# An output projection of 20 products of 171 columns in place of seven of 256, with new TensorE lists

## The chip, the cores and the metric

The kernel runs on one core of a Trainium2 chip. The metric is the time of one execution on the device in microseconds; the time of a kernel is the median of several runs. The core has a matrix engine (TensorE, PE in the profile; its weight loads have a row of their own, PEld), three engines for everything else (VectorE, DVE; ScalarE, ACT; GpSimd, POOL) and a queue that issues transfers (SyncE, SP). Each works through its own list of instructions in order and waits for the others by semaphores. [...]

## The reference, cut to what matters

The input x is 128 batches of 128 rows (tokens) and 512 columns, adj is 128 x 128. Layer 0 is a residual step and a norm. Layer 1 is masked attention with eight heads, an output projection and two norms. The change concerns `o @ w_proj + b_proj`:

```python
# layer 0 (W1 = W2 = adj): only the row maximum of A = adj @ x is needed beside x
pre = A[:, :, None, :] + (C - A)[:, :, :, None];  out = max(relu(pre), axis=-1)
x = layernorm(x + out)
# layer 1
qkv = (x @ w_qkv);  attn = softmax(mask(q k^T * scale));  o = attn @ v
o = o @ w_proj + b_proj                   # w_proj: 512 x 512
ln = (o - mean) * rsqrt(var + 1e-5) * gamma + beta
x = layernorm(x + o + ln)
```

All is float32.

## The kernel before

The 128 batches are worked off in 32 groups of four. A loop over p (from line 1482) walks through the groups in a software pipeline: step p does the scores S0 to S3 and the values product V of group p, the attention product A0 to A3 and the output projection O of group p - 1, the query and key product Q of group p + 1, and layer 0's product L of group p + 2. Tokens stand in columns, so a group's projection multiplies a 512 x 512 block (two halves of 256 tokens, four blocks of 128 rows) by a 512 x 512 weight.

Large products are not done plainly. Q and V use tables (`QK` and `VV`) of bilinear schemes: some sums of the left side are made by POOL (`token_sums`, tiles `hl`), the right side is replaced once by combined weights (`weight_forms`, line 776), and the class `Bilinear` (line 893) then runs "nodes". A node multiplies one or two sums by weight forms into a bank, adds earlier snapshots to it (DVE), seeds other banks with a copy of it (ACT, `k<-k`), keeps a snapshot in SBUF (`u<-k`), or writes a block of the result (DVE, the rest by POOL). The values product V takes 20 products of 171 columns, the projection O takes Strassen's seven products of 256 columns (`class Strassen`, `unit_sums`, `o_unit`, tiles `so` for the sums, `wp` for the weights). In O, ACT first copies the bias row into two banks, ACT keeps three snapshots, and DVE writes four result blocks `o`. A product of 171 columns has two matrix multiplications, one of Strassen's has four; in the trace each float32 multiplication is two instructions.

After O, `tails` does both norms of a group: DVE statistics, POOL roots and wide sums, ACT scalings, with the rows `xr` loaded back from memory.

Attention itself uses part of the array: in `scores` an operand has 64 rows (`k<-qk`, 64*128), in `attend` an output has 64 rows (`k<-s,v`, 128*64). All others use the full 128*128.

What sets the order: the lists `FIRST`, `STEP` and `LAST` fix TensorE's order in the first, middle and last step, token by token (`A2` is the attention of batch 2, `V5` node 5 of V, and so on). In `LAST`, B and R are attention and plain projection of the last group and T is the end of the group before it. All other engines' instructions, and SP's transfers, are ordered by a planner (class `Plan`), which has a cost for each operation, gives it a due time from TensorE's ideal times and picks the next one by due time. Buffers have fixed slots; a buffer waits for the readers of the one before it in its slot. `take` hands out the eight banks.

```python
STEP = """
A0 A1 A2 A3 S0 S1 S2 S3 V0 V1 V2 V3 V4 V5 V6 V7 V8 V9 V11 V10 V12 V13 V14 V15 L1 V16 V17 L0 O1 O2 O6
O5 O7 O4 Q0 L3 L2 O3 Q2 Q3 Q1 Q4 Q5 Q6 Q7 Q8 Q9 Q14 Q10 Q11 Q12 Q15 Q13 Q17 Q19 Q20 Q18 Q21 Q23 Q22
Q24 Q16 Q25
""".split()
```

Many helpers record instructions under one line: line 466 is every matrix multiplication, 460 every two-operand sum (DVE or POOL), 463 every scalar-tensor-tensor on DVE. Tile names then tell them apart.

Of the kernel before, what the change touches and what calls it, by code (L numbers as in the profile page):

```python
# [14 lines left out]
AX = mybir.AxisListType  # L15

# [189 lines left out]
)  # L206


STEP = """
A0 A1 A2 A3 S0 S1 S2 S3 V0 V1 V2 V3 V4 V5 V6 V7 V8 V9 V11 V10 V12 V13 V14 V15 L1 V16 V17 L0 O1 O2 O6  # L210
O5 O7 O4 Q0 L3 L2 O3 Q2 Q3 Q1 Q4 Q5 Q6 Q7 Q8 Q9 Q14 Q10 Q11 Q12 Q15 Q13 Q17 Q19 Q20 Q18 Q21 Q23 Q22
Q24 Q16 Q25
# [7 lines left out]

LAST = """
A2 V0 A0 A1 V2 V3 S0 V5 V1 A3 V6 S1 V4 S2 V7 V8 V10 V9 V11 V14 V13 O1 V12 O2 V16 O6 S3 O5 O7 V17 V15
O4 O3 B0 B1 T3 R0 B2 T1 R2 T0 B3 R1 T2 R3
# [12 lines left out]
class Buf:  # L236


    def __init__(self, plan, slot, make):
        self.slot, self.make, self.tile, self.log = slot, make, None, []  # L240
        self.before = plan.slots.get(slot)
        plan.slots[slot] = self
# [143 lines left out]
def kernel(  # L386
# [47 lines left out]
    def take(cols=512, add=False):  # L434


        if cols == 512:
            i = next(i for i in free if not add or i not in partial)
            partial.discard(i)
        else:  # L440
            i = next((i for i in list(free)[:-1] if i in partial), free[0])
            if not add:
                partial.add(i)
        free.remove(i)
        return bank(i)
# [9 lines left out]
    def small(kind, cols, bufs=8):  # L455
        i = small_n[kind] = small_n.get(kind, -1) + 1
        return buf(f"{kind}{i % bufs}", [P, cols])
# [318 lines left out]
    def weight_forms(table, dst, width, block, slots, cost, pool=False):  # L776
        made = {}
        per = 2 * D // width
        rooms = [buf(s, [P, per, width]) for s in slots]

        def operand(i):
            if i < table.blocks:
                return block(i)
            r, c = divmod(i - table.blocks, per)
            return rooms[r], c, lambda: rooms[r].t[:, c]

        def add(dst, dst_at, a, b, sa, sb_):
            (ba, ka, pa), (bb, kb, pb) = a, b
# [19 lines left out]
        def temp(i):  # L808
            if i < table.blocks or i in made:
                return  # L810
            made[i] = True
            a, b, s = table.temps[i - table.blocks]
            temp(a)
            temp(b)
            bt, c, ap = operand(i)
            add(ap, (bt, c), operand(a), operand(b), 1, s)

        for w, terms in enumerate(table.forms):
# [3 lines left out]
            if len(terms) == 1:  # L822
                ((i, s),) = terms
                b, k, ap = operand(i)
# [3 lines left out]
                    lambda ap=ap, form=form, s=s: pin(A.mul(form(), ap(), float(s))),  # L828
# [7 lines left out]
            for i, s in terms[2:]:  # L836
                add(form, at, (dst, w, form), operand(i), 1, s)
# [55 lines left out]
    class Bilinear:  # L893


        def __init__(self, table, left, form, width, rooms, costs, out, on_vector=False):
            self.table, self.left, self.form, self.width = table, left, form, width
            self.on_vector = on_vector
# [3 lines left out]
        def product(self, b, tok, w, start):  # L902
            bt, key, ap = self.left[tok]
# [10 lines left out]
            plan.add("PE", self.costs[0], emit, [(form, w), (bt, key)], [b])  # L914

        def node(self, n):
# [19 lines left out]
            if block is None:  # L936
# [3 lines left out]
                for m in seeds:  # L940
                    nb = self.banks[m] = take(2 * width, True)
                    plan.add("ACT", act, lambda nb=nb: pin(A.copy(cols(nb), cols(b))), [b], [nb])  # L942
# [75 lines left out]

    def weight_load(w, src, col):
        rows = src.rearrange("(d c p) e -> d p c e", d=2, p=P)  # L1020
        for i, d, c in ((0, 0, 0), (3, 0, HE), (1, 1, 0), (2, 1, HE)):
            dma(
                lambda i=i: w.t[:, i],
                lambda d=d, c=c: rows[d, :, :, ds(col + c, HE)],
                [],
                [(w, i)],
                256,
            )

    def weight_sums(w):  # L1030
        for i, a, b in ((4, 3, 0), (6, 2, 3), (5, 2, 4), (3, 1, 5)):
            plan.add(
                "POOL",
                1.3,
                lambda i=i, a=a, b=b: tt(GP, w.t[:, i], w.t[:, a], w.t[:, b], ALU.subtract),
                [(w, a), (w, b)],
                [(w, i)],
            )

    class Strassen:  # L1040


        def __init__(self, w, left, outs, us, bias=None):
            self.w, self.left, self.outs, self.us, self.bias = w, left, outs, us, bias
            self.banks, self.snaps = {}, {}

        def add(self, i, k):
            fresh = False
            if k not in self.banks:
                fresh = self.bias is None or k not in self.bias  # L1050
                b = self.banks[k] = take(add=not fresh)
                if not fresh:
                    src, row = self.bias[k]
                    plan.add("ACT", 0.5, lambda: pin(A.copy(halves(b), row())), [src], [b])
            b = self.banks[k]
            lb, key, ap = self.left[i]
            w = self.w

            def emit():
                left = ap()  # L1060
                for s in range(2):
                    for c in range(2):
                        mm(
                            halves(b)[:, s],
                            left[:, c, ts(s, P)],
                            w.t[:, i - 1, c],
                            fresh and s == 0 and c == 0,
                        )

            plan.add("PE", 1.725, emit, [(w, i - 1), (lb, key)], [b])  # L1070

        def snap(self, k):
            b = self.banks[0]
            u = self.snaps[k] = buf(self.us[k - 1], [P, 512])
            plan.add("ACT", 0.5, lambda: pin(A.copy(u.t, b.t)), [b], [u])

        def result(self, half, col, k, s):
            b, u = self.banks[k], self.snaps[s]
            dst, key, ap = self.outs[half, col]
            plan.add(  # L1080
                "DVE",
                0.61,
                lambda: tt(V, ap(), halves(b), u.t.rearrange("p (k n) -> p k n", k=2), ALU.add),
                [b, u],
                [(dst, key)],
            )

        def product(self, i):
            banks = self.banks
            self.add(i, (None, 0, 1, 2, 3, 2, 0, 0)[i])  # L1090
            if i in (1, 6, 7):
                self.snap((1, 6, 7).index(i) + 1)
            if i == 2:
                self.result(0, 0, 1, 1)
                give(banks[1])
            elif i == 7:
                give(banks[0])
                self.result(1, 1, 2, 3)
            elif i == 3:
                self.result(0, 1, 2, 2)  # L1100
                give(banks[2])
            if i in (4, 7) and 3 in banks and 3 in self.snaps:
                self.result(1, 0, 3, 3)
                give(banks[3])

    def unit_sums(a, s):
        for dst, p, q_, op in (
            (s[0], a[1][0], a[1][1], ALU.add),
            (s[1], s[0], a[0][0], ALU.subtract),
            (s[2], a[0][0], a[1][0], ALU.subtract),  # L1110
            (s[3], a[0][1], s[1], ALU.subtract),
        ):
            plan.add(
                "POOL",
                1.25,
                lambda dst=dst, p=p, q_=q_, op=op: tt(GP, dst[2](), p[2](), q_[2](), op),
                [p[:2], q_[:2]],
                [dst[:2]],
            )
        return {1: a[0][0], 2: a[0][1], 3: s[3], 4: a[1][1], 5: s[0], 6: s[1], 7: s[2]}  # L1120

    def o_unit(g, wp):
        a = [
            [(oT[g, h], None, lambda h=h, d=d: oT[g, h].t[:, ds(2 * d, 2)]) for d in range(2)]
            for h in range(2)
        ]
        rooms = [buf(f"so{i}", [P, 2, 2, HT]) for i in range(2)]
        s = [(rooms[i // 2], i % 2, lambda i=i: rooms[i // 2].t[:, i % 2]) for i in range(4)]
        left = unit_sums(a, s)
        for h in range(2):  # L1130
            os_[g, h] = buf(f"o{h}", [P, 2, D])
        outs = {
            (h, c): (os_[g, h], c, lambda h=h, c=c: os_[g, h].t[:, :, ds(c * HE, HE)])
            for h in range(2)
            for c in range(2)
        }
        bias = {
            0: (bp_bc, lambda: bp_bc.t[:, :HE].unsqueeze(1).to_broadcast([P, 2, HE])),
            2: (bd, lambda: bd.t.unsqueeze(1).to_broadcast([P, 2, HE])),
        }  # L1140
        return Strassen(wp, left, outs, ("u3", "u4", "u5"), bias)
# [177 lines left out]
    def tails(g):  # L1319
        mv = buf(f"mvo{g % 2}", [P, G, 2])  # L1320
        mz = buf(f"mvz{g % 2}", [P, G, 2])
        for j in range(G):
            o = os_[g, j // 2]
            bn(lambda o=o, j=j: o.t[:, j % 2], [o], mv, j)
        stat = finish(mv, range(G))
        rows = []
        for h in range(2):
# [5 lines left out]
            for j in range(2):  # L1333
                norm(
                    lambda z=z, j=j: z.t[:, j],
                    lambda o=o, j=j: o.t[:, j],
# [11 lines left out]
            plan.add("POOL", 2.34, lambda z=z, o=o: tt(GP, z.t, z.t, o.t, ALU.add), [z, o], [z])  # L1348
# [56 lines left out]
    def tail_before(b):  # L1405

        j = b % 2
# [196 lines left out]
```

## Time and profile before

| what | us |
| --- | --- |
| median of 3 runs | 1871.42 (1869.94 to 1871.91) |
| the profiled execution | 1872.38 |
| its span, first to last instruction | 1870.5 |
| PE busy, instructions | 1853.4 (99%), 12013 |
| DVE busy | 1357.2 (73%) |
| ACT busy | 1585.2 (85%) |
| POOL busy | 1440.9 (77%) |
| transfers, mean rate | 183 GB/s |

All times of the trace are counted from the span's start. A line of the timeline gives start, duration, engine, line of the code, operation, output and inputs by tile name, shapes and a count of like instructions that follow each other; a bracket at its end gives idle time ahead of it and what ended that. Matmuls overlap, so the duration of one is longer than the distance to the next. A line of the groups gives busy time and the mean of one.

### The profile page before, as it was taken

The page shows a single profiled execution, that of the slowest core. Times are in us where ns is not written, and L with a number is a line of the kernel's source. Part 1 is how long each engine was busy: PE and PEld are TensorE (multiplying, and loading weights), DVE is VectorE, ACT ScalarE, POOL GpSimd, SP SyncE. Part 2 cuts the span into 40 slices and gives each one's busy share as a digit, 9 for nine tenths or more (in the row PEclk, how much of TensorE's full clock was granted, in tenths as well). Part 3 has the DMA queues.
Part 4 walks back from the last instruction along what each step waited for, and adds up shares of the span by engine and source line. Part 5 has one row for each costly group of instructions (what it writes and reads, how often), then busy time and mean ns, then how long its engine had stood idle before and what let it go on. Part 6 is the DMA issues. An engine that isn't in the chain of part 4 may idle for free.

```text
span 1870.5 us, 37547 instructions
## 1 busy us (share of the span) xinstructions
PE 1853.4 (99%) x12013; PEld 1618.2 (87%) x12013; DVE 1357.2 (73%) x2524; ACT 1585.2 (85%) x4681; POOL 1440.9 (77%) x1546
## 2 busy tenths in 40 slices
PE   9999999999999999999999999999999999999997
PEld 7788988888988889888889888898888888888985
DVE  7677676777776777767777667777677776777668
ACT  4787888988889888889888898888898888988885
POOL 4658877788777788777887777977778877788774
PEclk9999999999999999999999999999999999999999
DMA  7654676557675566765576655667656676557564
GB/s 218 191 161 125 194 212 183 158 168 209 187 209 159 166 189 192 215 172 164 172 204 191 195 160 172 195 186 208 170 165 186 197 198 195 159 168 202 161 223 136
DMA packets 444388, 342.03 MB, mean 183 GB/s; under 512 B 276768, under 2 KB 377248, under 8 KB 444192
## 3 DMA queue, kind: packets, MB, share of 16 engines
q1 hardware_dynamic: 443904, 339.11, 63.2%
q8 instruction: 97, 1.59, 0.4%
q14 instruction: 99, 0.81, 0.1%
q10 hardware_dynamic: 288, 0.52, 0.1%
HBM read 172.82 MB, written 166.72 MB: 182 GB/s over the span
## 4 chain that ended last, share of the span: by engine, by line
PE 95%; ACT 1%; DVE 1%; DMA 1%; POOL 1%; issue 0%; SPq 0%; POOLq 0%; ACTq 0%
PE k L466 95%; DMA xr<-spill 1%; ACT s L1205 0%; ACT s L1234 0%; DVE st L583 0%; POOL xr L460 0%; POOL wqk L460 0%; ACT u L948 0%; ACT k L942 0%; POOL rs L460 0%; ACT xr L654 0%; ACT z L654 0%; DVE k L463 0%; DVE x L460 0%; PE k L728 0%
## 5 line engine op out<-in xcount | busy, mean ns | idle before, releaser
L466 PE MATMUL k<-hl,wqk 128*128 128x256 f32 x2232 | 517.9, 379 | 2.3 <-POOL hl L460 1.3
L466 PEld LDWEIGHTS k<-hl,wqk 128*128 128x128 f32 x2232 | 423.8, 190 | 62.2 <-POOL hl L460 2.4
L1205 ACT ACTIVATE s<-s,nm 128x128 f32<-128x128 f32 x1024 | 400.3, 397 | 2.3 <-DVE nm L1196 2.3
L1234 ACT ACTIVATE s<-s,rec 128x128 f32<-128x128 f32 x1008 | 323.1, 395 | 0.0
L948 ACT COPY u<-k 128x512 f32<-128x512 f32 x551 | 284.1, 529 | 32.3 <-PE k L466 23.3
L942 ACT COPY k<-k 128x512 f32<-128x512 f32 x372 | 192.0, 516 | 137.5 <-PE k L466 129.6
L466 PE MATMUL k<-wv,hl 128*128 128x171 f32 x1736 | 277.4, 310 | 1.1 <-ACT u L948 1.1
L466 PEld LDWEIGHTS k<-wv,hl 128*128 128x128 f32 x1736 | 258.2, 189 | 20.2 <-issue 14.3
L1246 DVE STREAM_TRANSPOSE pu<-s 128x1024 f32<-128x1024 f32 x128 | 159.3, 1245 | 131.9 <-ACT s L1234 131.8
L466 PE MATMUL k<-x1T,wqk 128*128 128x256 f32 x992 | 244.3, 379 | 0.0
L463 DVE SCALAR_TENSOR_TENSOR qk<-k,u 128x512 f32<-128x512 f32 x248 | 169.6, 687 | 101.9 <-PE k L466 48.2
L460 POOL TENSOR_TENSOR x<-x,be_bc 128x1024 f32<-128x1024 f32 x62 | 146.8, 2368 | 108.9 <-DVE xt L689 107.5
L466 PE MATMUL k<-wp,so 128*128 128x256 f32 x992 | 224.6, 379 | 0.0
L466 PEld LDWEIGHTS k<-wp,so 128*128 128x128 f32 x992 | 188.3, 190 | 38.2 <-issue 13.4
L463 DVE SCALAR_TENSOR_TENSOR s<-k,mask 128x512 f32<-128x512 f32 x256 | 156.7, 683 | 82.2 <-PE k L466 82.2
L466 PEld LDWEIGHTS k<-x1T,wqk 128*128 128x128 f32 x992 | 188.5, 190 | 25.6
L1205 ACT ACTIVATION_READ_ACCUMULATOR s<-s,nm 128x1 f32 x1024 | 199.0, 194 | 0.0
L460 POOL TENSOR_TENSOR z<-z,ga_bc 128x1024 f32<-128x1024 f32 x60 | 142.6, 2376 | 42.4 <-ACT z L654 42.2
L466 PE MATMUL k<-wp,oT 128*128 128x256 f32 x744 | 170.9, 379 | 0.0
L466 PEld LDWEIGHTS k<-wp,oT 128*128 128x128 f32 x744 | 141.2, 190 | 31.4 <-issue 6.9
L460 POOL TENSOR_TENSOR hl<-x1T,hl 128x256 f32<-128x256 f32 x217 | 158.0, 745 | 3.1 <-DMA x1T<-xhop 3.1
L1196 DVE TENSOR_REDUCE nm<-s 128x8 f32<-128x1024 f32 x128 | 152.4, 1213 | 0.1
(155 smaller groups left out, 3325.7 us busy)
## 6 DMA issues: line engine op xcount, KB each, us to landing
hop<-pu SPq DMA_DIRECT2D x128, 512.0 KB, 3.0
s<-hop SPq DMA_DIRECT2D x512, 128.0 KB, 3.5
spill<-x SPq DMA_DIRECT2D x62, 512.0 KB, 4.9
xhop<-xt SPq DMA_DIRECT2D x248, 128.0 KB, 4.3
x1T<-xhop SPq DMA_DIRECT2D x248, 128.0 KB, 4.6
x<-in_x_dram SPq DMA_DIRECT2D x60, 512.0 KB, 5.3
xr<-spill SPq DMA_DIRECT2D x60, 512.0 KB, 6.5
out_dram<-xr SPq DMA_DIRECT2D x60, 512.0 KB, 4.7
```

The lines of the kernel that those rows point to most:

```text
L460: pin(eng.tensor_tensor(dst, a, b, op))
L463: pin(V.scalar_tensor_tensor(dst, a, s, b, op0, op1))
L466: pin(PE.matmul(dst, lhsT=lhsT, rhs=rhs, start=start, stop=True, skip_group_check=True))
L942: plan.add("ACT", act, lambda nb=nb: pin(A.copy(cols(nb), cols(b))), [b], [nb])
L948: plan.add("ACT", act, lambda: pin(A.copy(cols(u), cols(b))), [b], [u])
L1196: lambda: pin(V.tensor_reduce(nm.t, flat(), AX.X, ALU.max, negate=True)),
L1205: A.activation(flat()[:, i], flat()[:, i], AF.Exp, bias=nm.t[:, i : i + 1], accum_out=sm.t[:, i : i + 1],)
L1234: A.activation(flat()[:, i], flat()[:, i], AF.Identity, scale=rec.t[:, i : i + 1])
L1246: V.transpose(u.t.rearrange("p q h b -> p h q b"), flat().rearrange("p h (q a) -> p h q a", q=Q),)
```

## The change

The output projection gets a bilinear scheme of its own. Table `OO` has 18 nodes with 20 products of 171 columns; the 512 columns are padded to 513 with a zero. Its 14 left sums (`O_SUMS`) are made by POOL in the class `Sums`, in ten rooms of the tiles `so`: ten sums can be made at once, and a room is reused when its last reader has been planned. `Bilinear` runs the nodes with its snapshots copied by DVE, as it did before for V of the last group only. The biases no longer start two banks by an ACT copy: where a node seeds one of three banks (2, 6 and 9), DVE adds the bias, or a difference of its column blocks, in the copy. These differences are in the slots `adj_sb` and `ident`.

The projection of group 30 (the last but one) is now done in the last step by `project`, plainly, four batches of four multiplications of 512 columns with the raw weights (`U0` to `U3`), with the ends of `tail` in place of `tail_before`. `STEP` serves the steps 1 to 29, the new list `NEXT` step 30, and `LAST` step 31; all are new, `FIRST` is unchanged. `tails` of a group follow its last O node.

`w_proj` is loaded in four transfers into the slots `z` and `xr0`, and its 20 forms are made in the first step. In `weight_forms` a temporary that is itself a form is made in its final place, for Q and V too, which takes copies away. Small tiles turn in rings of 6 for 8, and `take` prefers a partly used bank that isn't the last free one.

```diff
 STEP = """
-A0 A1 A2 A3 S0 S1 S2 S3 V0 V1 V2 V3 V4 V5 V6 V7 V8 V9 V11 V10 V12 V13 V14 V15 L1 V16 V17 L0 O1 O2 O6
-O5 O7 O4 Q0 L3 L2 O3 Q2 Q3 Q1 Q4 Q5 Q6 Q7 Q8 Q9 Q14 Q10 Q11 Q12 Q15 Q13 Q17 Q19 Q20 Q18 Q21 Q23 Q22
-Q24 Q16 Q25
+A0 V0 A2 A3 V3 A1 S1 S3 S0 S2 V4 V2 V1 V10 V5 V7 V6 V8 V9 V11 O0 V13 V12 O1 O2 V15 L0 O4 O3 V14 V16
+L3 O6 O7 V17 O8 O5 O10 Q0 O9 O17 O12 Q2 O13 Q3 O14 L2 O11 O16 L1 Q4 O15 Q1 Q5 Q9 Q6 Q8 Q7 Q14 Q10
+Q12 Q17 Q11 Q19 Q13 Q20 Q21 Q23 Q18 Q25 Q22 Q24 Q15 Q16
 """.split()
+NEXT = """
+V0 A2 A0 S0 S2 A1 A3 V3 V1 V4 V2 S1 V10 V5 V6 V8 V7 V9 V11 V12 V13 V15 O1 O0 V14 V16 O2 O3 O5 O4 O6
+O7 O8 V17 O9 O11 O10 O17 O12 O14 Q0 O16 S3 Q2 Q3 Q4 O15 O13 Q1 Q5 Q7 Q9 Q10 Q6 Q8 Q17 Q11 Q14 Q15
+Q12 Q19 Q13 Q16 Q20 Q21 Q18 Q23 Q25 Q22 Q24
+""".split()
 LAST = """
-A2 V0 A0 A1 V2 V3 S0 V5 V1 A3 V6 S1 V4 S2 V7 V8 V10 V9 V11 V14 V13 O1 V12 O2 V16 O6 S3 O5 O7 V17 V15
-O4 O3 B0 B1 T3 R0 B2 T1 R2 T0 B3 R1 T2 R3
+A0 V2 A2 V0 S2 S0 A1 V5 U2 V1 V4 V3 A3 V6 V8 V7 V10 S3 V9 U1 V11 V14 V13 V17 S1 V12 V16 U0 V15 U3 B0
+B2 R0 R2 B3 R3 B1 R1
 """.split()
...
-    def small(kind, cols, bufs=8):
+    def small(kind, cols, bufs=6):
...
             if type(self.left) is not list:
+                self.left.used(tok)
...
                 for m in seeds:
                     nb = self.banks[m] = take(2 * width, True)
-                    plan.add("ACT", act, lambda nb=nb: pin(A.copy(cols(nb), cols(b))), [b], [nb])
+                    if m in self.bias:
+                        src, row = self.bias[m]
+                        plan.add(
+                            "DVE", dve, lambda nb=nb, row=row: tt(V, pair(nb), pair(b), row(), ALU.add), [b, src], [nb]
+                        )
+                    else:
+                        plan.add("ACT", act, lambda nb=nb: pin(A.copy(cols(nb), cols(b))), [b], [nb])
...
+    class Sums:
+        def fill(self):
+            while self.order and self.room:
+                i = self.order.pop(0)
+                r, c = self.room.popleft()
+                a, b, s = O_SUMS[i - 8]
...
+                plan.add(
+                    "POOL",
+                    0.71,
+                    lambda ap=ap, pa=pa, pb=pb, s=s: tt(
+                        GP, ap(), pa(), pb(), ALU.add if s > 0 else ALU.subtract
+                    ),
...
+        def read(self, i):
+            self.reads[i] -= 1
+            if i >= 8 and not self.reads[i]:
+                self.room.append(self.got[i][:2])
+        def used(self, i):
+            self.read(i)
+            self.fill()
...
+        costs = (0.58, 0.42, 0.46, 0.87)
+        return Bilinear(OO, Sums(blocks, OO.nodes), wp, VB, ["u3", "u4", "u5"], costs, out, True, bias)
...
-        step = FIRST if p == 0 else STEP if p < NG - 1 else LAST
+        step = FIRST if p == 0 else STEP if p < NG - 2 else NEXT if p < NG - 1 else LAST
...
-            elif kind == "T":
-                tail_before(a - G + n)
+            elif kind == "U":
+                project(a - G + n, False, *again)
...
-                o = o or o_unit(p - 1, wp)
-                o.product(n)
-                if n == 3 and p < NG - 1:
+                o = o or o_unit(p - 1)
+                o.node(n)
+                if i == last["O"]:
                     tails(p - 1)
...
-                wp = buf("wp", [P, 7, 2, HE])
-                weight_load(wp, w_proj, 0)
-                weight_sums(wp)
+                wo_raw = [buf(s, [P, 2, 3 * VB]) for s in ("z", "xr0")]
...
+                wp = buf("wp", [P, 20, VB])
+                weight_forms(OO, wp, VB, o_block, ("xr1",), 0.37, True)
```

## The prediction

> **What bounds the kernel now.** I read the busy rows of the page first, then the chain of work that ended last, then TensorE's (PE's) timeline in one middle step, then its timeline near the end.
>
> ```profile
> PE 1853.4 (99%) x12013; PEld 1618.2 (87%) x12013; DVE 1357.2 (73%) x2524; ACT 1585.2 (85%) x4681; POOL 1440.9 (77%) x1546
> ...
> PE 95%; ACT 1%; DVE 1%; DMA 1%; POOL 1%; issue 0%; SPq 0%; POOLq 0%; ACTq 0%
> ```
>
> PE is busy for 99% of the span at a granted clock of 0.998, and 95% of the last chain is PE. The others have room on average (DVE 27%, POOL 23%, ACT 15%). So a change counts first by the time it adds to PE's own queue, and by another engine only where PE has to wait for it. One middle step, PE alone (start, duration, instruction, number of them):
>
> ```profile
> 660.33 3.71 PE L466 MATMUL k<-s,v 128*64 128x128 f32 x64
> 663.97 3.84 PE L466 MATMUL k<-qk 64*128 64x128 f32 x64
> ...
> 673.09 4.82 PE L466 MATMUL k<-wv,hl 128*128 128x171 f32 x32
> 677.74 0.75 PE L466 MATMUL k<-wv,x1T 128*128 128x171 f32 x4
> ...
> 681.21 3.62 PE L466 MATMUL k<-wp,oT 128*128 128x256 f32 x16
> 684.66 5.34 PE L466 MATMUL k<-wp,so 128*128 128x256 f32 x24
> 689.84 1.89 PE L466 MATMUL k<-wp,oT 128*128 128x256 f32 x8
> ```
>
> No line shows an idle time: starts follow starts, and the next step begins at 717.55, 57.22 us later. Durations overlap (an instruction's 379 ns runs into the next), so I price by differences of starts. From 681.21 to 689.84 are 40 instructions: **0.216 us per 256-column instruction**. From 673.09 to 677.74 are 32: **0.145 us per 171-column instruction**. Each product of the code has two (171 columns) or four (256) matrix multiplications, and each of these is two instructions in the trace.
>
> The next view, from the last steps, prices something the middle step hides:
>
> ```profile
> 1806.13 1.09 PE L466 MATMUL k<-s,v 128*64 128x128 f32 x16
> 1807.16 0.85 PE L466 MATMUL k<-wv,hl 128*128 128x171 f32 x4
> 1807.93 1.97 PE L466 MATMUL k<-s,v 128*64 128x128 f32 x32
> 1809.83 1.43 PE L466 MATMUL k<-wv,x1T 128*128 128x171 f32 x8
> 1811.19 1.16 PE L466 MATMUL k<-qk 64*128 64x128 f32 x16
> ```
>
> `s,v` (attention times values) and `qk` (scores) use half of the array, 128*64 or 64*128. By starts, `s,v` runs of 16, 32 and 64 take 1.03, 1.90 and 3.64 us: 0.054 per instruction plus 0.16 per run. A run of four 171-column instructions between half-array runs takes 0.77 where 4 x 0.145 = 0.58; a run of eight takes 1.36 where 8 x 0.145 = 1.16: 0.19 more per run. So a product put between two half-array runs costs 0.19 + 0.16 = **0.35 us** more than the same product among others of its kind.
>
> **The change, part by part.**
>
> *The products.* A group's output projection goes from 7 products (56 instructions of 256 columns, 56 x 0.2158 = 12.08 us) to 20 (80 of 171, 80 x 0.1454 = 11.63): 0.45 us less. Thirty groups: **-13.5 us**. Group 30 goes plain in the last step: 4 batches x 8 instructions of 512 columns; the row with four from 692.43 to 694.15 gives 0.43 each, so 13.73 against 12.08: **+1.65**.
>
> [...] The groups list has LDWEIGHTS at 190 ns; were that the spacing, a group would take 80 x 0.190 = 15.2 us, 3.1 more, and the kernel 30 x 3.1 = 94 us more. But the value products already run every 145 ns with loads of 189 ns listed, so the loads overlap and I keep 0.145.
>
> *The new TensorE lists.* STEP had `A0 A1 A2 A3 S0 S1 S2 S3 V0`: half-array work in one block. Now it has `A0 V0 A2 A3 V3 A1 S1 S3 S0 S2 V4`: V0 and V3, one product each, stand between half-array runs. Counted over the whole built order, the changes from full to half array go from 44 to 103: 58 from 29 steps, two more from NEXT, one fewer in LAST. 59 x 0.35 = **+20.6 us**, and two scores-to-attention changes at 0.16, +0.3. [...] By a count of products alone (0 per change) the sum is near 1861; by the row it is near 1882. I take the row, since the excess is alike at every such place in that view. The price could be lower where weights are loaded early, down to half (the half-array side alone, 0.16: +9.4), and I see no reason for above 0.40.
>
> *The other engines, per group of 57.2 us.* POOL: four sums of 1.29 become 14 of 0.744 (the row of the `hl` sums) and one added `o<-o,u` (0.865, the `v<-v,u` row): +6.1 us. DVE: four `o<-k,u` of 0.691 become seven snapshot copies (0.499), six outputs (0.511), one bank sum and three bias adds (0.517): +5.9. ACT loses two bias copies and three snapshots (0.59), gains two bank copies (0.431): -2.1. Against the same step before:
>
> ```profile
> 659.80:717.02 57.22, 57.22 (x377) 50.60 (x376) 41.64 (x78) 49.92 (x148) 45.45 (x48) 1.00 0.66 185
> ```
>
> (after PE and its loads: DVE, ACT, POOL), DVE goes to 47.5 (83%), ACT to 47.9, POOL to 51.6 (90%). All fit, so they cost nothing while PE's order hides them. The cover is thin in places: a product now waits for its POOL sum (ten of 14 have a room at once, four wait until an earlier product has released one), for ACT's bank copy, or three times for DVE's bias add, which stands behind row maxima (1.21) and statistics (0.68) in DVE's queue; every later product is queued behind such a product, and its outputs, `tails` and the next sums wait for it. Such waits are absent in the middle step of before. Bounds per step: 0, and one row maximum's length (1.2) late, 29 x 1.2 = 35 us. I take near nothing, **+0.5** in all, since the same kinds of wait in V and Q leave PE without a gap.
>
> *The first group.* The `wp` weights are now 20 forms: some 19 POOL sums of about 0.55 (`wv<-wp,z` rows) for four of 1.28, +5.3, with six on DVE and three on ACT; still four loads on SP's queue. They land in a stretch where POOL is nearly full (from 83.25 to 118.3 it idles for 3.4 us):
>
> ```profile
> 98.66 1.29 POOL L460 TENSOR_TENSOR wp<-wp 128x512 f32<-128x512 f32 x1
> 101.58 0.73 POOL L460 TENSOR_TENSOR hl<-x1T 128x256 f32<-128x256 f32 x1 [1.64 <-PE k L466]
> ```
>
> With the sums of that step POOL has 10 us more before Q's sums are done. None of it may reach PE (the norm's additions, 2.37 each, can stand back), or 8 us may; **+2.5**. The forms of Q and V lose copies on ACT; PE runs unbroken beside them, so nothing. The shorter rings of small tiles (8 to 6) can delay only 0.2 us statistics: nothing.
>
> *The end.* The last PE instruction starts its run so, and DVE comes late to it:
>
> ```profile
> 1847.64 3.70 PE L466 MATMUL k<-wqk,oT 128*128 128x512 f32 x8 [0.79 <-ACT oT L1295]
> ...
> 1852.30 7.13 PE L466 MATMUL k<-wqk,oT 128*128 128x512 f32 x16
> ...
> 1861.45 0.69 DVE L583 BATCH_NORM_STATS2 st<-k 128x6 f32<-128x512 f32 x1
> ```
>
> PE is done at 1859.43, DVE reads at 1861.45, some 1.8 us of backlog from group 30's tails. These now start earlier, beside V, and a single projection stands last: **-1.8**. `B3 R3 B1 R1` makes two projections wait for their attention copies (0.79 each) where before had that wait once and one of 0.51: **+0.3**.
>
> *The sum.* -13.5 + 1.65 + 20.6 + 0.3 + 0.5 + 2.5 - 1.8 + 0.3 = +10.5. The profiled execution took 1872.38 us (span 1870.5 and 1.9 around it); the median of the three runs, 1871.42, lies 0.96 lower. I add to the median: **1882 us**.
>
> **The rivals.**
>
> 1. *Other engines fall behind* (likely place: POOL at 90%, or DVE where V and the projection meet). For it: POOL waits in order, 3.6 us for a transpose and 4.0 for statistics each step; if those stayed, 51.6 + 7.6 = 59.2 would exceed the step. Against: those waits are for things due at a fixed time, and shrink when POOL comes later. At half a microsecond per step: 1882 + 15 = 1897.
> 2. *Faster: the changes of array mode don't cost here.* One mechanism: the loads for the product after a half-array run are pulled ahead so that 0.35 vanishes; the kernel gets faster once a change costs (10.5 + 3.7)/59 = 0.24 us less than 0.35, so below 0.11 us. For it: the price comes from a few places at the end, where other waits exist. Against: those runs have no idle time listed and scale evenly. Time: 1882 - 20.6 = 1861.
> 3. *Half price*: 1882 - 11.2 = 1871, no change.
>
> **How the numbers follow.** Main case 0.62 (its own range 1876 to 1889), rival 1 0.18, rival 2 0.10, rival 3 0.10. A difference under 0.2% (3.7 us) is about what a measurement of this kernel can't tell from none. Rival 3 is half within that and a quarter on either side; the main case and rival 1 are slower: faster 0.12, same 0.06, slower 0.82. The range 1868 to 1897 leaves out rival 2 and half of rival 1.
>
> **What would show it.** In the changed profile: `wp` instructions every 0.145 us; a middle step near 57.45 us (57.22 - 0.45 + 2 x 0.35 = 57.47); V runs of four between `s,v` runs at 0.77 us; no idle time before PE's lines in a middle step; POOL near 51 of a step. The prediction is wrong if the step is near 56.8 (no price of mode changes), or if PE's lines carry idle times released by POOL `so` or DVE `k`.

## The result, and the profile after

| | before | after |
| --- | --- | --- |
| median, four runs each | 1870.97 us (1869.94 to 1871.91) | 1882.9 us (1882.33 to 1883.47) |
| span of the profiled execution | 1870.5 | 1881.0 |
| PE instructions | 12013 | 12709 |
| one middle step | 57.22 | 57.43 |

The kernel became slower: ratio 1.0064, 95% interval 1.0046 to 1.0081. The busy rows of the page after and the engines' shares of the chain that ended last:

```profile
PE 1864.1 (99%) x12709; PEld 1644.7 (87%) x12709; DVE 1480.2 (79%) x2921; ACT 1529.6 (81%) x4577; POOL 1587.2 (84%) x1878
...
PE 96%; DVE 1%; ACT 1%; DMA 1%; issue 0%; SPq 0%; POOL 0%; POOLq 0%; DVEq 0%; ACTq 0%
```

POOL and DVE have 146 and 123 us more to do, and PE is still busy for 99% of the span. TensorE's timeline at the beginning of step 1 shows the half-array work with V0 and V3 between its runs:

```profile
87.94 1.09 PE L567 MATMUL k<-s,v 128*64 128x128 f32 x16
88.96 0.85 PE L567 MATMUL k<-wv,hl 128*128 128x171 f32 x4
89.74 1.97 PE L567 MATMUL k<-s,v 128*64 128x128 f32 x32
91.64 0.85 PE L567 MATMUL k<-wv,x1T 128*128 128x171 f32 x4
92.41 1.10 PE L567 MATMUL k<-s,v 128*64 128x128 f32 x16
93.44 3.84 PE L567 MATMUL k<-qk 64*128 64x128 f32 x64
```

By starts the V runs take 0.78 and 0.77 us, the attention runs 1.02, 1.90 and 1.03. A middle step as a row (length, then busy time of PE, its loads, DVE, ACT, POOL, granted clock as a share of full speed, DMA share, GB/s), and below it 5.5 us near the end:

```profile
660.00:717.43 57.43, 57.43 (x401) 51.53 (x400) 45.51 (x91) 48.22 (x145) 50.58 (x58) 1.00 0.65 185
1825.50:1831.00 5.50, 5.48 (x28) 5.17 (x29) 3.39 (x7) 4.92 (x13) 1.42 (x3) 0.50 0.34 134
```

The first is close to the forecast of 57.47 us. The second was not forecast: the granted clock is 0.50. The timeline there:

```profile
1821.09 1.32 PE L567 MATMUL k<-wv,x1T 128*128 128x171 f32 x8
1825.52 1.98 PE L567 MATMUL k<-s,v 128*64 128x128 f32 x16 [3.11 <-DMA s<-hop]
1827.43 1.51 PE L567 MATMUL k<-wv,hl 128*128 128x171 f32 x4
1828.73 2.49 PE L567 MATMUL k<-wv,x1T 128*128 128x171 f32 x8
1831.01 0.96 PE L567 MATMUL k<-wv,hl 128*128 128x171 f32 x4
```

A3 of the last list (the attention of batch 123) waits 3.11 us for its weights `s`, which come back from memory, and the three runs behind the wait take 5.49 us. Where the wait is gone (below) the same three take 2.87, so the clock costs 2.6 more. Two projections R further on wait for their attention copies, 0.69 us each where the prediction had 0.79.

The spans differ by 10.5 us. By stage, with step 30 counted from its first product (A0 before, V0 after):

| stage | forecast | measured |
| --- | --- | --- |
| start to step 1 | 0 | -0.1 |
| steps 1 to 29 | 29 x (-0.45 + 0.70), first group 2.5, waits 0.5: +10.2 | +4.3 |
| steps 30 and 31 | -0.45 + 1.65 + 0.35, two scores changes 0.3, `B R` waits 0.3: +2.1 | +7.4 |
| after the last PE instruction starts | -1.8 | -1.1 |
| sum | +10.5 | +10.5 |

So the total is right and two of its parts are not, by about 6 and 5 us in opposite directions. Of the 7.4 us, 1.8 are more listed idle time of TensorE and 2.6 the clock.

### The profile page after: what moved, and what is told of

Read it like the earlier page. It is cut to its first block, busy times and chain, and to the rows that moved or that the text cites. A ratio compares the mean times of both kernels' runs of the same rounds, so it can differ in the third digit from the quotient of the medians.

```text
span 1881.0 us, 39653 instructions
## 1 busy us (share of the span) xinstructions
PE 1864.1 (99%) x12709; PEld 1644.7 (87%) x12709; DVE 1480.2 (79%) x2921; ACT 1529.6 (81%) x4577; POOL 1587.2 (84%) x1878
## 4 chain that ended last, share of the span: by engine, by line
PE 96%; DVE 1%; ACT 1%; DMA 1%; issue 0%; SPq 0%; POOL 0%; POOLq 0%; DVEq 0%; ACTq 0%
PE k L567 96%; DMA s<-hop 0%; ACT s L1307 0%; DMA wqk<-in_L_gnn_w_proj_dram 0%; SPq L571 0%; DVE st L684 0%; ACT s L1278 0%; DVE wp L564 0%; DVE pu L1319 0%; POOL rs L561 0%; DVE k L561 0%; ACT k L1064 0%; PE k L829 0%; DVE u L1068 0%; DVE wqk L561 0%
## 5 line engine op out<-in xcount | busy, mean ns | idle before, releaser
L1070 ACT COPY u<-k 128x512 f32<-128x512 f32 x551 | 288.6, 530 | 89.9 <-PE k L567 46.6
L1064 ACT COPY k<-k 128x512 f32<-128x512 f32 (+1 forms) x432 | 217.2, 503 | 159.4 <-PE k L567 148.2
L1307 ACT ACTIVATE s<-s,rec 128x128 f32<-128x128 f32 x1008 | 311.8, 390 | 1.4 <-DVE rec L1289 1.4
L567 PE MATMUL k<-wp,so 128*128 128x171 f32 x1680 | 292.9, 308 | 0.7 <-DVE u L1068 0.7
L567 PE MATMUL k<-wv,hl 128*128 128x171 f32 x1736 | 292.4, 310 | 0.1
L567 PEld LDWEIGHTS k<-wp,so 128*128 128x128 f32 x1680 | 262.4, 189 | 32.2 <-issue 27.6
L1278 ACT ACTIVATION_READ_ACCUMULATOR s<-s,nm 128x1 f32 x1024 | 194.3, 190 | 0.0
L1068 DVE COPY u<-k 128x342 f32<-128x342 f32 x217 | 108.5, 506 | 45.0 <-PE k L567 43.7
L561 POOL TENSOR_TENSOR hl<-x1T 128x256 f32<-128x256 f32 x186 | 135.2, 727 | 10.0 <-DMA x1T<-xhop 8.0
```

What stands on the lines that cost most here:

```text
L561: pin(eng.tensor_tensor(dst, a, b, op))
L567: pin(PE.matmul(dst, lhsT=lhsT, rhs=rhs, start=start, stop=True, skip_group_check=True))
L1068: plan.add("DVE", dve, lambda: pin(V.tensor_copy(cols(u), cols(b))), [b], [u])
L1070: plan.add("ACT", act, lambda: pin(A.copy(cols(u), cols(b))), [b], [u])
L1278: A.activation(flat()[:, i], flat()[:, i], AF.Exp, bias=nm.t[:, i : i + 1], accum_out=sm.t[:, i : i + 1],)
L1307: A.activation(flat()[:, i], flat()[:, i], AF.Identity, scale=rec.t[:, i : i + 1])
```

## The experiments

My theory: a product between two half-array runs costs 0.35 us, 58 times in the middle steps; without it the new projection would be a gain. Rivals: the price lies in other engines (POOL, DVE) that now do more, or in something else that came with the new lists. For the last step: A3 is late because of transfers, because of its softmax, or because any order of it is held by other engines.

**Half-array work in one block again** (the changed kernel, one list):

```diff
 STEP = """
-A0 V0 A2 A3 V3 A1 S1 S3 S0 S2 V4 V2 V1 V10 V5 V7 V6 V8 V9 V11 O0 ...
+A0 A2 A3 A1 S1 S3 S0 S2 V0 V2 V1 V3 V4 V5 V7 V10 V6 V8 V9 V11 O0 ...
```

> The kernel after, with V0 and V3 moved behind the scores in STEP, so that attention and scores stand in one block again (the next V nodes are reordered a little for their seeds); all else as after. If changes between full and half array cost what the prediction says (0.35 us for each product put between), each of 29 steps loses 2 x 0.35 = 0.70 us: step 57.43 to 56.73, kernel 1882.9 - 20.3 = 1862.6. If the projection's other work (POOL, DVE) is what lengthened the step, it stays at 57.4 and the kernel at 1883. At half the price: 1873.

Measured: 1861.19 us (1860.74 to 1861.39), ratio to before 0.995, interval 0.9935 to 0.9965. Its middle step:

```profile
655.93:712.66 56.73, 56.73 (x401) 51.55 (x400) 45.16 (x90) 47.23 (x144) 49.30 (x58) 1.00 0.68 191
```

The step falls by 0.70, twice 0.35, with the same products, sums and copies on POOL and DVE (the V nodes behind V3 stand in a slightly different order). That is 29 x 0.70 = 20.3 of the 21.7 us; the rest is in the last steps. Against before (57.215 on average over undisturbed steps) the step is 0.485 shorter: that is the whole product saving, so the added work of POOL and DVE costs a middle step nothing. This kernel beats both.

**The same two places in the kernel before:**

```diff
 STEP = """
-A0 A1 A2 A3 S0 S1 S2 S3 V0 V1 V2 ...
+A0 V0 A1 A2 V1 A3 S0 S1 S2 S3 V2 ...
```

> The kernel before, with V0 and V1 put between its attention products (A0 V0 A1 A2 V1 A3) in STEP, nothing else. Price of array changes: 30 steps x 0.70 = +21.0, 1871 to 1892, step 57.22 to 57.92, with no idle time listed on PE. If the price belongs to the last step's waits alone: no change, 1871.

Measured: 1910.25 us, ratio 1.0211 (1.0195 to 1.0226); a step takes 58.35, 1.14 more. TensorE's timeline, then one line of its weight loads:

```profile
673.06 0.85 PE L466 MATMUL k<-wv,hl 128*128 128x171 f32 x4
673.84 1.97 PE L466 MATMUL k<-s,v 128*64 128x128 f32 x32
675.74 0.85 PE L466 MATMUL k<-wv,hl 128*128 128x171 f32 x4
676.52 1.09 PE L466 MATMUL k<-s,v 128*64 128x128 f32 x16
677.54 4.29 PE L466 MATMUL k<-qk 64*128 64x128 f32 x64
681.76 2.01 PE L466 MATMUL k<-wv,x1T 128*128 128x171 f32 x12
```

```profile
680.67 0.96 PEld L466 LDWEIGHTS k<-qk 64*128 64x128 f32 x14 [0.16 <-DVE s L463]
```

The V runs take 0.78 each, as in the changed kernel: 0.70 for the two. The other 0.44 is new: the 64 scores take 4.22 us by starts instead of 3.77. The loads of the last 14 wait until one of DVE's masks is done. I take this as a wait for a bank (a tile `k`): V0 and V1, moved ahead, hold banks while the scores are written. That is argued from the order of the list; for it speaks that with L in the same places (below), which needs its banks for a shorter time, the scores take 3.77 again. So the price is confirmed. My total (1892) was 18 us too low: 13 of them (30 x 0.44) are this wait, which I had left out. The profiled execution, at 1906.92 the fastest of the four, is explained by the steps (30 x 1.14 = 34.2 of 34.6 us); why the median lies 3 us above it is not.

**Attention and scores in turn, no product between them** (the kernel before):

```diff
 STEP = """
-A0 A1 A2 A3 S0 S1 S2 S3 V0 ...
+A0 S0 A1 S1 A2 S2 A3 S3 V0 ...
```

> The kernel before, with attention and scores alternating in STEP (A0 S0 A1 S1 A2 S2 A3 S3), no product between them, so six more changes between the 128*64 and 64*128 shapes and none more to the full array. If any change of the array's shape costs (0.16 us by the run of 64 in the middle step): 30 x 6 x 0.16 = +29, 1871 to 1900. If only changes to and from the full array cost: 1871.

Measured: 1907.03 us, ratio 1.0194 (1.0179 to 1.021); a step takes 58.41, 1.2 more.

```profile
671.99 1.09 PE L466 MATMUL k<-s,v 128*64 128x128 f32 x16
673.02 1.16 PE L466 MATMUL k<-qk 64*128 64x128 f32 x16
...
680.46 1.43 PE L466 MATMUL k<-wv,hl 128*128 128x171 f32 x8
```

From 671.99 to 680.46 are 8.47 us, where the block of before takes 3.64 + 3.77 = 7.41. That is 1.06 for six more changes, 0.18 each; the rest of the 1.2 is a short wait inside V. Going from one half-array shape to the other costs as much as going to the full array: 0.35 is two changes of shape, not something of the value product.

**Another full-array product in those places** (the kernel before, layer 0's product L in place of V):

```diff
 STEP = """
-A0 A1 A2 A3 S0 ... V15 L1 V16 V17 L0 O1 ...
+A0 L1 A1 A2 L0 A3 S0 ... V15 V16 V17 O1 ...
```

> The kernel before with L1 and L0, one product of 512 columns each, put between the attention products (A0 L1 A1 A2 L0 A3), nothing between the scores; they keep a bank for a short time only, unlike V0 and V1 of e2. If the price is that of a change of the array's shape, whatever the product: 30 steps x 0.70 = +21 (29 steps have L: +20.3), step 57.22 to 57.92, kernel 1871 to 1891. If e2's 1.14 us per step is the price of the changes themselves and not 0.70 plus a wait of the scores for a bank: +33, 1904. If it belongs to 171-column products: 1871.

Measured: 1963.44 us (1955.82 to 1967.16), ratio 1.0502 (1.0485 to 1.052).

```profile
694.02 1.09 PE L466 MATMUL k<-s,v 128*64 128x128 f32 x16
695.05 1.13 PE L466 MATMUL k<-x,adjT 128*128 128x512 f32 x2
696.10 1.97 PE L466 MATMUL k<-s,v 128*64 128x128 f32 x32
698.00 1.13 PE L466 MATMUL k<-x,adjT 128*128 128x512 f32 x2
699.06 1.09 PE L466 MATMUL k<-s,v 128*64 128x128 f32 x16
700.08 3.84 PE L466 MATMUL k<-qk 64*128 64x128 f32 x64
703.85 1.43 PE L466 MATMUL k<-wv,hl 128*128 128x171 f32 x8
```

In the block the price is the same: 6.06 us from 694.02 to 700.08, less 3.64 for attention and 2 x 0.86 for L, leaves 0.70. All else in the 93 us is a different thing: steps of 58 to 67 us, most of them with waits in V for ACT. The first early L waits 6.34 us for its x to be loaded, so layer 0 begins too early there; that this is behind the other steps too is not shown. As a time this run says nothing on array shapes, and as a forecast (1891) it missed. Two of its waits in V are of use further down, with a row of 3.3 and one of 3.5 us behind them (the number before the DMA share is the granted clock):

```profile
233.24 3.14 PE L466 MATMUL k<-wv,hl 128*128 128x171 f32 x12 [1.68 <-ACT u L948]
1372.43 2.16 PE L466 MATMUL k<-wv,hl 128*128 128x171 f32 x12 [2.65 <-ACT u L948]
...
234.50:237.80 3.30, 3.30 (x13) 3.30 (x13) 2.49 (x6) 3.28 (x14) 3.13 (x5) 0.50 0.00 0
1372.50:1376.00 3.50, 3.25 (x20) 2.85 (x20) 3.50 (x6) 3.46 (x15) 3.43 (x4) 1.00 0.00 0
```

**The last step: three of four reloaded row blocks behind the attention weights' loads** (the changed kernel):

```diff
-                dma(r, lambda s=s: s.t, [s], [(lastw, b // 2)])
+                op = dma(r, lambda s=s: s.t, [s], [(lastw, b // 2)])
+                if i != 2:
+                    op.preds.add(loads[G * g - 1])
```

> The kernel after, with three of the four 512 KB row loads of the last step issued on SP's queue behind the four loads of the transposed attention of batch 123, nothing else. If that attention came late because its transfers shared the DMA engines with the 3 MB of the last step's loads, and the half clock behind it (0.50 for some 5 us) is a consequence of the 3.1 us of idleness, both go: -3.1 - 2.3 = -5.4, to 1877.5. If the half clock comes from elsewhere: -3.1, to 1879.8. If the scores of batch 3 are simply too late in NEXT: no change, 1882.9.

Measured: 1881.59 us (1879.96 to 1882.21), ratio 1.0058 (1.0041 to 1.0075). A3 waits 2.01 us in place of 3.11. The write of the attention weights to memory (`hop<-pu`) took 7.7 us to land in the changed kernel, and still 7.5 here: the 1 MB of raw `w_proj` and one block of 512 KB were issued just ahead of it. The median of such writes over the whole trace is 2.9. The queue's lines in the changed kernel, then those of the kernel before:

```profile
1809.87 0.40 SPq L571 DMA_DIRECT2D wqk<-in_L_gnn_w_proj_dram  x1
1810.31 0.50 SPq L571 DMA_DIRECT2D wqk<-spill  x1
1812.30 0.33 SPq L571 DMA_DIRECT2D hop<-pu  x1
1820.02 1.74 SPq L571 DMA_DIRECT2D s<-hop  x4
```

```profile
1801.46 0.34 SPq L470 DMA_DIRECT2D hop<-pu  x1
1807.24 0.40 SPq L470 DMA_DIRECT2D wqk<-in_L_gnn_w_proj_dram  x1
```

So the large loads are not new: the kernel before has the same 1 MB and four blocks of 512 KB in its last step. New is that the write comes behind them, 2.5 us after the step's start (1809.77) in place of 4.7 us ahead of it (1806.13). In the new list the scores S3 of step 30 start 32.9 us into the step; before, all four scores were written within the first 7.4.

**U1 ahead of A3** (the blocked kernel, to give A3 more time):

```diff
-A0 V2 A2 V0 S2 S0 A1 V5 U2 V1 V4 V3 A3 V6 V8 V7 V10 S3 V9 U1 V11 ...
+A0 V2 A2 V0 S2 S0 A1 V5 U2 V1 V4 V3 U1 A3 V6 V8 V7 V10 S3 V9 V11 ...
```

> e1 with one token of LAST moved: U1, 3.4 us of plain projection, stands ahead of A3 and not behind V9. In e1 PE waits 2.5 us for A3's operand and runs 3.3 us at half clock behind it (1.7 us lost). If the half clock is a consequence of the wait, both go: -4.2, 1861.2 to 1857.0. If the clock drops for another reason: -2.5, to 1858.7. If U1's own end (statistics, DVE) then holds something else up, less.

Measured: 1861.33 us (1859.67 to 1862.76), ratio 0.995 (0.9935 to 0.9964). A3 waits for nothing and the clock is full, yet the last step, from its first attention product to the start of the last PE instruction, is as long as without the edit (59.7 against 59.5). What came in its place:

```profile
1804.87 1.09 PE L567 MATMUL k<-s,v 128*64 128x128 f32 x16
1805.90 0.85 PE L567 MATMUL k<-wv,hl 128*128 128x171 f32 x4
1806.59 1.32 PE L567 MATMUL k<-wv,x1T 128*128 128x171 f32 x8
1807.74 0.74 PE L567 MATMUL k<-wv,hl 128*128 128x171 f32 x4
1808.81 1.48 PE L567 MATMUL k<-qk 64*128 64x128 f32 x16 [0.33 <-DVE u L1068]
...
1812.73 2.59 PE L567 MATMUL k<-wv,hl 128*128 128x171 f32 x16 [1.07 <-ACT k L1064]
1816.51 0.85 PE L567 MATMUL k<-wv,hl 128*128 128x171 f32 x4 [1.19 <-DVE u L1068]
...
1838.94 3.70 PE L567 MATMUL k<-wqk,oT 128*128 128x512 f32 x8 [1.70 <-ACT oT L1368]
```

V now waits for DVE's and ACT's copies, and the first R a microsecond longer for its attention copy. The waits shown add up to 4.3 us; without the edit A3's 2.53 and the slow clock stood there.

**S3 of step 30 earlier** (the blocked kernel, S3 behind O17 in place of O16):

```diff
-O7 O8 V17 O9 O11 O10 O17 O12 O14 Q0 O16 S3 Q2 ...
+O7 O8 V17 O9 O11 O10 O17 S3 O12 O14 Q0 O16 Q2 ...
```

> e1 with one token of NEXT moved: S3, the scores of batch 3 of group 30 (A3's source), four nodes earlier (behind O17 instead of O16), some 3 us of PE time. If A3 is late because its scores stand late in the list: the wait of 2.5 us and the half clock go, -4.2, to 1857.0. If ACT's queue (the wide norms that stand ahead of its exponentials) decides when its softmax is done: no change, 1861.2.

Measured: 1861.16 us (1860.96 to 1861.91), ratio 0.995 (0.9935 to 0.9964). The write goes out 0.6 us after the last step's start in place of 2.5, and takes 9.0 us to land. A3's wait is 1.24, the clock behind it stays full, and the last step is 1.1 shorter; step 30 is 1.2 longer, so nothing is gained.

**All reloads behind the write, U2 behind A3**, once in the blocked kernel and once in the changed one:

```diff
-A0 V2 A2 V0 S2 S0 A1 V5 U2 V1 V4 V3 A3 V6 ...
+A0 V2 A2 V0 S2 S0 A1 V5 V1 V4 V3 A3 U2 V6 ...
-        dma(wl, lambda: w_proj.rearrange("(c p) e -> p c e", p=P), [], [(lastw, "w")], 1024)
+        op = dma(wl, lambda: w_proj.rearrange("(c p) e -> p c e", p=P), [], [(lastw, "w")], 1024)
+        op.preds.add(sent[G * g - 1])
...
-                dma(r, lambda s=s: s.t, [s], [(lastw, b // 2)])
+                op = dma(r, lambda s=s: s.t, [s], [(lastw, b // 2)])
+                op.preds.add(sent[G * g - 1])
```

> The blocked list of the fastest kernel so far, with the projection weights and the four spilled row blocks of the last step ordered behind the write of batch 123's attention weights to memory (which takes 6.9 us to land there, where 2.6 is usual), and U2 behind A3 in the last list. If those transfers make A3 late: the write lands in 3 to 4 us, A3 waits for under 1 us, no half clock, and the time is 2.5 + 2.0 less 1 us lower, about 1857.7. If the last step is held by VectorE and ScalarE in any case: A3's wait goes, other waits come in its place, 1861.2. If the softmax on ScalarE makes A3 late: its wait stays near 2.5 or grows, since A3 now stands 3.4 us earlier, and the time is 1861 or more.

> The changed kernel with the same edit to its last step alone (weights and spilled blocks behind the write of batch 123's attention weights, U2 behind A3). Transfers make A3 late: the write lands in 3 to 4 us in place of 7.7, A3 waits under 1 us in place of 3.1, no half clock: 1882.9 - 2.3 - 2.6 = 1878.0. Other engines hold the last step: 1882.9. Softmax late: 1882.9 or more, A3's wait 3 us or more.

Measured: blocked 1862.97 us (1862.75 to 1863.12), ratio 0.9963 (0.9949 to 0.9977); changed 1884.14 us (1880.82 to 1884.44), ratio 1.0072 (1.0057 to 1.0087). In the changed kernel with this edit:

```profile
1820.72 1.09 PE L567 MATMUL k<-s,v 128*64 128x128 f32 x16
...
1840.07 1.51 PE L567 MATMUL k<-wv,hl 128*128 128x171 f32 x4 [2.89 <-DVE u L1068]
```

A3 now comes 4.8 us earlier in the trace and waits for nothing; the write was issued at 1806.12, landed in 2.7 us, and its loads were issued from 1808.94 on. But a value product further down waits 2.89 us for a snapshot copy, and then the clock is 0.50 there. What that copy stood behind is in DVE's timeline, which has no gap from 1834.90 on:

```profile
1834.90 0.70 DVE L684 BATCH_NORM_STATS2 st<-k 128x6 f32<-128x512 f32 x1 [0.24 <-PE k L567]
1835.51 1.21 DVE L561 TENSOR_TENSOR s<-s,rec 128x1024 f32<-128x1024 f32 x1
1836.64 0.68 DVE L561 TENSOR_TENSOR wqk<-wqk,k 128x512 f32<-128x512 f32 x1
1837.23 1.24 DVE L1319 STREAM_TRANSPOSE pu<-s 128x1024 f32<-128x1024 f32 x1
...
1839.51 0.51 DVE L1068 COPY u<-k 128x342 f32<-128x342 f32 x1
```

Of the lines shown, the first and the third are `tail` of a batch of group 30 (statistics, sum), the second and fourth are softmax. In the blocked kernel the last step did become 2.3 us shorter (57.2 for 59.5), but step 30 became 3.4 longer, with new waits of 1.62 and 1.24 for ACT's snapshots. The write goes out 6.2 us earlier (1806.12 for 1812.30 in the changed pair): the planner has put the softmax ahead of these snapshots. In the blocked kernel with this edit ACT's eight softmax scalings (2.46 us from 1784.25 on) stand just ahead of the snapshots that TensorE waits for until 1787.23.

So A3's wait goes when the write lands sooner and goes out sooner; this edit did both, and does not separate them. By the changed kernel's trace the slow landing alone (7.7 for 2.9 us, 4.8 more) is longer than the wait of 3.11. But taking the wait away does not give back what it costs. The last two steps together, from step 30's first attention product to the start of the last PE instruction, take 116.4 us in the changed kernel, 114.6 with the row blocks behind, 118.0 with all reloads behind; in the blocked kernel 114.7, and 114.9, 114.8 and 115.7 with its three edits. Only the first gained (1.8 us); the others moved the wait to DVE, to ACT or, with S3 earlier, to the load of the raw weights (0.96 us). What the last steps would take under a planner with other due times was not tried and stays open.

## Why the prediction was right, and which steps of it were not

**The price of the lists: right.** The forecast step was 57.47, it is 57.43; V runs of four take 0.77 to 0.78; no line of a middle step shows idle time. Undoing the two places gives back 0.70 per step, putting them into the kernel before costs 0.70, and so does another product in the same places. Rival 2 and rival 3 (free, or half price) are out. One change of shape costs 0.18 us (1.06 us for six more, with attention and scores in turn).

**The products: right, a little undersized.** -0.45 per group was forecast, the blocked kernel shows -0.485. The loads of 189 ns don't set the spacing of the `wp` products, as the prediction chose: eight of these instructions take 1.16 us by starts (690.22 to 691.38), 0.145 each.

**The other engines in a middle step: right.** POOL went to 50.58 for a forecast of 51.6, DVE to 45.51 for 47.5, ACT to 48.22 for 47.9. Rival 1 is out for the middle steps: the blocked kernel keeps all that work and loses only the shape changes. The +0.5 for such waits measured 0.

**The first group: wrong, +2.5 measured 0.** Step 1 takes 57.43 like the rest and shows no wait, although POOL's busy time in it goes up by 9.6 us, from 37.5 to 47.1. The term was read from POOL's stretch up to 118 us, which is nearly full; over the whole step POOL had room.

**What was in the profile of before and not in the sum.** The steps 1 to 29 of before took 1661.1 us, 1.9 more than 29 undisturbed steps, and its step 30 has 2.3 us of idle time of its own (1.25, 0.38 and 0.70):

```profile
1077.66 2.01 PE L466 MATMUL k<-wv,hl 128*128 128x171 f32 x12 [0.98 <-ACT u L948]
...
1782.82 1.10 PE L466 MATMUL k<-hl,wqk 128*128 128x256 f32 x4 [1.25 <-POOL hl L460]
```

The prediction took one middle step for all. After has none of these in steps 1 to 29 and 0.95 us in step 30.

**The last two steps: wrong, +2.1 measured +7.4.** Their terms, "Group 30 goes plain in the last step: +1.65" with the changes of shape of `NEXT` and `LAST`, counted PE's instructions alone. They had no term for when A3's weights come back from memory: the write that A3 depends on goes out behind 1 MB and 512 KB of loads (3.1 us of idle time), and behind that idle time the granted clock was 0.50 (2.6 us). That S3 stands late in step 30 is a part of it: S3 four nodes earlier took 1.9 us off the write's delay. About 1 us more is in none of the listed waits. None of the four changes of the lists could use the time; where the traces were followed, softmaxes and the `tail`s of group 30 then stood ahead of snapshots on ACT and DVE. DVE is busy for 51.6 of the last 61 us, but that is no larger a share than the 46.2 of 53.3 before, so its load alone does not tell the kernels apart, and what an order for these two steps could reach stays open. I had looked at DVE at the very end only, where the gain was forecast too large (-1.8, measured -1.1).

Against the sum the middle steps came out 5.9 us lower: -1.0 (29 steps at +0.215 for +0.25), -0.5 (waits), -2.5 (first group) and -1.9 (the idle time of before). The last two steps came out 5.2 higher and the end 0.7. That these cancelled, and the total came out within 1 us, is luck; the sign is not, because of the 20 us of the lists, which were measured by themselves.

## What to carry to other kernels

Count the places where the array's shape changes as well as the products: here 58 products between half-array runs (20 us) took more than the whole new scheme saved (about 14), and the same scheme in one block is 0.5% faster than before. Whoever moves a product ahead of a block must ask which banks it holds and what its inputs need: beside the change of shape that cost 0.44 us a step in one experiment and up to 9 us a step in another. In the last steps of a pipeline, where fewer products cover the other engines, a sum of TensorE's instructions is a lower bound: in four of five edits, shortening one wait there only brought out others. And an order has to be read for when its transfers go out: the same loads stood behind the write before the change, without a wait of A3, and ahead of it after, with a wait of 3.11 us.

## What the runs showed of the hardware

A change between two half-array shapes (128*64 to 64*128) costs 0.18 us (1.06 us for six), as much as one to the full array (0.35 us for two); I had forecast 0.16 for it.

The granted clock fell after four idle times in the last step. Behind 3.11 us in the changed kernel it was 0.50 from 1825.50 to 1831.00, and behind 2.89 us in the changed kernel with all reloads behind the write it was 0.50 from 1840.00 to 1846.00. Behind 2.53 us in the blocked kernel the mean from 1804.80 to 1809.50 was 0.64, and behind 2.01 us with three row blocks behind the loads the mean from 1824.70 to 1830.00 was 0.68. It stayed at 1.00 behind 1.24 us with S3 earlier (1805.50 to 1808.50) and behind 1.70 us with U1 ahead of A3 (1838.90 to 1842.80). The length alone does not decide: with L in V's place it was 0.50 behind 1.68 us and 1.00 behind 2.65 us (the lines above). What else decides, no run here shows.

A write of 512 KB, 2.9 us in the median of its 128 places, took 7.7 in the changed kernel behind a load of 1 MB and a block of 512 KB, and 2.7 where those were ordered behind it.
